# Layer 0's opening: keys first, values and the next keys placed behind the scores

## Chip, core and metric

The kernel runs on one core of one Trainium2 chip. The time is device microseconds for one launch of the whole program; before the change the median of three runs was 2810.7 us (2809.99 to 2813.46).

## What is computed

`x` is 4096 x 256, `adj` is 4096 x 4096, all float32. Four layers follow each other, and after each of them `x` becomes the layer norm of `x` plus the layer's output. The change touches layer 0 alone, an attention with four heads whose scores get the adjacency as a bias and as a mask:

```python
qkv = x @ Wqkv + bqkv                         # 256 -> 3 * 256, then q, k, v
scores = jnp.einsum('hnd,hmd->hnm', qh, kh) * SCALE
scores = scores + graph_bias * adj_matrix[None, :, :]
scores = jnp.where(attn_mask[None, :, :] == 0, jnp.float32(-1000000000.0), scores)
attn = jax.nn.softmax(scores, axis=-1)        # attn_mask is adj as well
out = jnp.einsum('hnm,hmd->hnd', attn, vh)
x = _layernorm(x + (out @ Wout + bout), axis=-1)
```

Layer 1 is a graph attention, layers 2 and 3 are products with the normalised adjacency.

## The kernel before

**Tiles.** Layer 0 goes through 32 row blocks of 128 rows (`Rows`), and for each through two pairs of heads (`Pair`). A pair is a unit; the 4096 keys are four stretches of 1024 columns, so a unit has four steps and the layer 256 (`step(t)`, L462). The program runs in the order in which it is written (`tc.manual_schedule()`, L651): each engine takes its instructions in that order, and what they wait for are semaphores that follow from the data and the buffers.

**A step** issues the scores of unit t // 4, stretch t % 4 (`score`, L361: eight matmul passes into two PSUM tiles, then on VectorE two passes that add the bias, write `z` and keep the maximum, L375); four steps later the exponentials on ScalarE (`expo`, L389); five steps later the transposes on TensorE and their copy out of PSUM on ScalarE (`turn`, L399); six steps later the product with the values (`attend`, L416). So steps 0 to 5 fill a pipeline and the full step begins at t = 6.

**The bias** of the next row block is made beside this, half a tile in a step: `load` (L251) brings a raw tile of 1024 x 128 of `adj` by four DMAs on SP's queue into one of two `raw` buffers; `make_bias` (L264) is three VectorE instructions (transpose, mask, scale and add); `make_edges` (L283) writes the transposed tile as bf16 `mk` (L289, ScalarE, with the row sum; two `mk` buffers) and sends it to DRAM as `edge` from POOL's queue (L295), for layer 1. `fetch` (L299) loads a row block's columns of x transposed, `xq`, and its rows, `xr`; `begin` (L308) makes its queries `qT` (L313 on TensorE, L321 on VectorE).

**Keys and values.** `load_x(mb)` (L197) loads one of eight blocks of 512 columns of x transposed (`xt`, pool of five buffers, which the transposed probabilities use later). `project(mb)` (L204) makes from it the keys of both pairs (L210, eight matmul passes, ScalarE evicts each into `store`, L217) and the values (L226, 16 passes, VectorE adds the bias and evicts, L233), then loads block mb + 4. Keys use the PSUM tiles `po0` and `po1`, one bank each; `begin` uses `po1` too, and the values share the one `tr` tile with the transposes.

**The opening** (L651 to L674) loads x block 0, the key and value weights, raw tile 0 of row block 0, x block 1, raw tile 1, `xq` and `xr`, then two x blocks more; makes the first queries; and then, over four stretches, makes the whole bias of row block 0, with `project(0)` and `project(1)` after the first two. In steps 1, 2 and 3 two further projections, keys and values, stand ahead of the step's score (L478 to L480).

Of the kernel before, what the change touches and what calls it, by code (L numbers as in the profile page):

```python
# [17 lines left out]
N = 4096  # L18
# [8 lines left out]
NS = N // TS  # L27
# [17 lines left out]
def tile_gnn(  # L45
# [123 lines left out]
    with ExitStack() as l0:  # L169
# [25 lines left out]
        x_in = {}  # L195

        def load_x(mb):  # L197
            xt = pp_.tile([P, 2, 512], F32, tag="pt", name="xt")
            nc.sync.dma_start(
                xt, xT[:, mb * 512 : (mb + 1) * 512].rearrange("(c p) m -> p c m", p=P)  # L200
            )
            x_in[mb] = xt

        def project(mb):  # L204

            xt = x_in.pop(mb)
            for pr in range(2):
                pk = ps_o.tile([P, 512], F32, tag=f"po{pr}", name="pk")
                for cc in range(2):
                    nc.tensor.matmul(  # L210
                        pk,
                        wkv_sb[:, cc, pr * P : (pr + 1) * P],
                        xt[:, cc, :],
                        start=(cc == 0),
                        stop=(cc == 1),
                    )
                nc.scalar.activation(  # L217
                    kT[:, pr, mb * 512 : (mb + 1) * 512],
                    pk,
                    AF.Identity,  # L220
                    bias=bqk_sb[:, 2 + pr : 3 + pr],
                )
            pv = ps_t.tile([P, 4, D], F32, tag="tr", name="pv")
            for s in range(4):
                for cc in range(2):
                    nc.tensor.matmul(  # L226
                        pv[:, s, :],
                        xt[:, cc, s * P : (s + 1) * P],
                        wkv_sb[:, cc, D : 2 * D],
                        start=(cc == 0),  # L230
                        stop=(cc == 1),
                    )
            nc.vector.tensor_tensor(  # L233
                v_sb[:, mb * 4 : (mb + 1) * 4, :],
                pv,
                bv_b.unsqueeze(1).to_broadcast([P, 4, D]),
                ALU.add,
            )
            if mb + 4 < N // 512:
                load_x(mb + 4)  # L240

        class Rows:

# [212 lines left out]
        rows = [Rows(ib) for ib in range(NCH)]  # L456
# [5 lines left out]
        def step(t):  # L462
            unit, k = divmod(t, NS)
            ib, pr = divmod(unit, 2)
            live = t < n_steps
            ua, ka = divmod(t - LA, NS)
            tag_a, tag_o = f"po{ua % 2}", f"po{1 - ua % 2}"
            ut, kt = divmod(t - LT, NS)
            ue, ke = divmod(t - LE, NS)
            attends = 0 <= ua < n_units  # L470
            turns = 0 <= ut < n_units
            expos = 0 <= ue < n_units
            grow = live and ib + 1 < NCH
            if grow and pr == 0 and k == NS - 1:
                rows[ib + 1].fetch()
            if ua > 0 and ka == 0:
                pairs[ua - 1].scale()
            if t > 0:  # L478
                for mb in range(2 * t, min(2 * t + 2, N // 512)):
                    project(mb)  # L480
            if live:
                if k == 0:
                    pairs[unit] = Pair(rows[ib], pr)
                pairs[unit].score(k)
            if expos:
                pairs[ue].expo(ke, 0)
            if turns:
                pairs[ut].turn(kt, 0)
            if expos:
                pairs[ue].expo(ke, 1)  # L490
            if attends:
                pairs[ua].attend(ka, tag_a)
                if ka == NS - 2:
                    pairs[ua].sums()
                if ka == NS - 1:
                    pairs[ua].norm(tag_o)
            if ua > 0 and ka == 1:
                if ua % 2 == 0:
                    pairs[ua - 1].rows.finish(tag_o)
                del pairs[ua - 1]  # L500
            if grow:
                if pr == 1 and k == NS - 2:
                    rows[ib + 1].begin(tag_o if attends else "po1")
                kb, half = divmod(pr * NS + k, 2)
                if edges:
                    edges.pop().make_edges()
                edges.append(rows[ib + 1])
                rows[ib + 1].make_bias(kb, half)
                if half == 0 and kb + 1 < NS:
                    rows[ib + 1].load(kb + 1)  # L510
                elif half == 0 and ib + 2 < NCH:
                    rows[ib + 2].load(0)
            elif edges:
                edges.pop().make_edges()
            if turns:
                pairs[ut].turn(kt, 1, by_dve=not live)
            for f, *args in tail.get(t, ()):
                f(*args)
# [98 lines left out]
        def first_es():  # L617
# [30 lines left out]
                (first_es,),  # L648
            ],
        }  # L650
        with tc.manual_schedule():  # L651
            load_x(0)
            nc.sync.dma_start(wkv_sb, wqkv[:, D:].rearrange("(c p) e -> p c e", p=P))
            rows[0].load(0)
            load_x(1)
            rows[0].load(1)
            rows[0].fetch()
            load_x(2)
            load_x(3)
            nc.scalar.dma_start(wout_sb, wout.rearrange("(c p) e -> p c e", p=P))  # L660
            nc.scalar.dma_start(bout_b, bout.partition_broadcast(P))
            rows[0].begin("po1")
            for k in range(NS):
                for half in range(2):
                    rows[0].make_bias(k, half)
                    rows[0].make_edges()
                if k < 2:
                    project(k)
                if k + 2 < NS:
                    rows[0].load(k + 2)  # L670
                elif k + 2 == NS:
                    rows[1].load(0)
            for t in range(n_steps + LA + 2):
                step(t)  # L674

# [446 lines left out]
```

## Time and profile before

| what | value |
|---|---|
| median of three runs | 2810.7 us (2809.99 to 2813.46) |
| the profiled execution's own time | 2810.3 us |
| its span, first to last instruction | 2808.5 us |
| TensorE busy | 2740.4 us (98%) |
| VectorE busy | 2234.3 us (80%) |
| ScalarE busy | 1615.1 us (58%) |
| POOL busy | 234.2 us (8%) |
| mean granted TensorE clock | 0.991 |
| SP, raw tile piece, 128 KB: issue to landing | 3.9 us median over the run, 2.7 to 6.7 in the first 90 us |
| SP, x block, 512 KB: issue to landing | 5.3 us median, 4.4 to 6.0 |

Times come from one profiled execution, in microseconds from the first instruction. The granted clock is the share of TensorE's full speed. `PE` is TensorE's matmuls, `PEld` its weight loads, `DVE` is VectorE, `ACT` ScalarE, `SPq` the issue of DMAs by SP. In a timeline the bracket at the end of a line is the idle time of the engine before it, and who ended it. The chain of waits is followed back from the last instruction to what released it, and so on to the start. Matmul passes are counted one by one: one float32 product in the program is two of them.

### The profile page before, as it was taken

To read this page: it belongs to the slowest core of one execution; us is meant where nothing else is said; L and a number is where in the kernel's file an instruction comes from. 1 tells how busy PE (TensorE), PEld (TensorE's weight loads), DVE (VectorE), ACT (ScalarE), POOL (GpSimd) and SP (SyncE) were. 2 spreads that over 40 slices of the span, in tenths; PEclk is the share of its full clock that TensorE was granted. 3 is DMA by queue.
4 is the path that set the end of the run, shared out by engine and by line. 5 is a ranking of instruction groups with operands and counts; after the bars stand their busy time and mean duration, and the time that the engine had idled before them with its cause. 6 is when DMAs were issued, how large, how long until landed. Compare 5 with 4: busy or idle time off the path is not lost.

```text
span 2808.5 us, 58032 instructions
## 1 busy us (share of the span) xinstructions
PE 2740.4 (98%) x23664; PEld 1870.2 (67%) x23664; DVE 2234.3 (80%) x4091; ACT 1615.1 (58%) x2483; POOL 234.2 (8%) x404
## 2 busy tenths in 40 slices
PE   6999999999999999999998999999999999999997
PEld 4677777777777777777777888887444444444443
DVE  4799999999898999999758888885876568666565
ACT  2699999999999999999855655653100001000000
POOL 1111111111111111111100000000200000000000
PEclk9999999999999999999998999999999999999999
DMA  6344444444444444444362222212555545555552
GB/s 157 61 86 85 87 92 85 88 86 88 90 87 82 90 91 82 86 92 89 100 188 68 76 73 70 76 46 72 177 157 173 163 154 163 164 160 179 180 169 76
DMA packets 671291, 308.01 MB, mean 110 GB/s; under 512 B 547376, under 2 KB 577456, under 8 KB 671024
## 3 DMA queue, kind: packets, MB, share of 16 engines
q1 hardware_dynamic: 655776, 265.10, 38.4%
q0 software_dynamic: 13440, 37.77, 3.5%
q8 instruction: 185, 3.03, 0.5%
q10 hardware_dynamic: 1808, 1.44, 0.2%
q14 instruction: 82, 0.67, 0.1%
HBM read 258.21 MB, written 46.01 MB: 108 GB/s over the span
## 4 chain that ended last, share of the span: by engine, by line
PE 96%; DVE 2%; ACT 1%; DMA 1%; issue 1%; SPq 0%; DVEq 0%; ACTq 0%
PE m L950 27%; PE po L423 17%; PE po L775 16%; PE sc L366 16%; PE ptr L405 10%; PE py L984 2%; PE pq L313 1%; PE pp L335 1%; PE pb L441 1%; PE pk L210 1%; PE pv L226 1%; PE sc L137 1%; PE pm L744 0%; SPq L256 0%; DMA xt<-in_xT 0%
## 5 line engine op out<-in xcount | busy, mean ns | idle before, releaser
L375 DVE CUSTOM_DVE_ANT_0 z<-sc,bias 128x1024 f32<-128x1024 f32 x512 | 605.8, 1220 | 40.5 <-PE sc L366 38.9
L391 ACT ACTIVATE z<-z,nm 128x1024 f32<-128x1024 f32 x512 | 590.2, 1153 | 6.7 <-DVE nm L387 6.7
L413 ACT COPY pt<-ptr 128x1024 f32<-128x1024 f32 x507 | 511.3, 1008 | 99.2 <-PE ptr L405 89.3
L366 PE MATMUL sc<-store,qT 64*128 64x512 f32 x2048 | 507.0, 608 | 1.4 <-DVE mx L375 1.3
L423 PE MATMUL po<-pt,xc 128*64 128x128 f32 x8192 | 504.1, 276 | 0.0
L775 PE MATMUL po<-store,pt 128*128 128x257 f32 x2048 | 459.5, 382 | 3.6 <-DVE pt L765 3.6
L423 PEld LDWEIGHTS po<-pt,xc 128*64 128x64 f32 x8192 | 442.1, 137 | 17.6 <-DVE pt L411 0.2
L405 PEld LDWEIGHTS ptr<-ident,z 64*128 64x128 f32 x8192 | 322.3, 138 | 177.6 <-issue 78.4
L775 PEld LDWEIGHTS po<-store,pt 128*128 128x128 f32 x2048 | 385.0, 190 | 62.9 <-issue 3.6
L950 PE MATMUL m<-asum,ysum 128*128 128x512 f32 x768 | 357.0, 595 | 6.3 <-issue 6.3
L405 PE MATMUL ptr<-ident,z 64*128 64x64 f32 x8192 | 356.5, 225 | 5.8 <-ACT pt L413 4.4
L366 PEld LDWEIGHTS sc<-store,qT 64*128 64x128 f32 x2048 | 192.9, 189 | 119.7 <-issue 109.4
L950 PEld LDWEIGHTS m<-asum,ysum 128*128 128x128 f32 x768 | 146.1, 190 | 177.9 <-issue 160.2
L950 PE MATMUL m<-asum,store 128*128 128x512 f32 x512 | 263.1, 596 | 0.0
L724 ACT ACTIVATE z<-z,es_q 128x1024 f32<-128x1024 f32 x128 | 147.1, 1149 | 183.2 <-DVE mx L711 178.9
L950 PE MATMUL m<-a,ysum 128*128 128x512 f32 x512 | 245.3, 592 | 0.0
L295 POOL DMA_DIRECT2D edge<-mk x256 | 145.3, 568 | 1004.5 <-ACT mk L289 981.0
L956 ACT COPY e<-m 128x512 f32<-128x512 f32 x32 | 18.5, 586 | 351.3 <-PE m L950 351.3
L919 DVE TENSOR_TENSOR asum<-a 128x512 f32<-128x512 f32 x128 | 88.0, 687 | 163.7 <-PE m L950 163.7
L278 DVE SCALAR_TENSOR_TENSOR bias<-rt,gb,u 128x512 f32<-128x512 f32 x256 | 194.1, 758 | 9.1
L950 PEld LDWEIGHTS m<-asum,store 128*128 128x128 f32 x512 | 97.8, 191 | 123.6 <-issue 121.9
L272 DVE STREAM_TRANSPOSE rt<-raw 128x512 f32<-128x512 f32 x256 | 179.6, 702 | 0.0
(126 smaller groups left out, 2544.5 us busy)
## 6 DMA issues: line engine op xcount, KB each, us to landing
a<-in_adjT SPq DMA_DIRECT2D x256, 512.0 KB, 5.1
raw<-in_adjT SPq DMA_DIRECT2D x512, 128.0 KB, 3.9
edge<-mk POOLq DMA_DIRECT2D x256, 128.0 KB, 2.5
mk<-edge SPq DMA_DIRECT2D x256, 128.0 KB, 2.9
xt<-in_xT SPq DMA_DIRECT2D x8, 512.0 KB, 5.3
xq<-in_xT SPq DMA_DIRECT2D x32, 128.0 KB, 3.8
xr<-in_x SPq DMA_DIRECT2D x32, 128.0 KB, 3.0
x<-xs POOLq DMA_DIRECT2D x8, 512.0 KB, 4.0
```

The source lines that it names most:

```text
L272: nc.vector.transpose(rt.rearrange("p (b r) -> p b r", r=QB), self.raw_now[:, half * nb : (half + 1) * nb, :],)
L278: nc.vector.scalar_tensor_tensor(self.bias[k][:, m0 : m0 + HT], rt, gb, u, ALU.mult, ALU.add)
L295: nc.gpsimd.dma_start(edge[self.ib * P : (self.ib + 1) * P, k * TS + m0 : k * TS + m0 + HT], mk)
L366: nc.tensor.matmul(ps[j][:, q * 512 : (q + 1) * 512], self.rows.qT[j * HD : (j + 1) * HD, self.pr, :], kT[j * HD : (j + 1) * HD, self.pr, ...
L375: nc.vector.tensor_tensor_reduce(z, ps[j], self.rows.bias[k], 1.0, NEG, ALU.add, ALU.max, self.mx[:, j, k : k + 1],)
L391: nc.scalar.activation(z, z, AF.Exp, bias=self.nm[:, j : j + 1], accum_out=self.ls[:, j, k : k + 1],)
L405: nc.tensor.transpose(pa[:, r, c, :], z[half, c * P : (c + 1) * P], ident[half, half])
L413: nc.scalar.copy(to, pa)
L423: nc.tensor.matmul(self.po[j * HD : (j + 1) * HD, 0:P], v_sb[:, ci, h * HD : (h + 1) * HD], self.pt[j][k][:, c, :], start=(ci == 0), stop= ...
L724: nc.scalar.activation(self.z[s], self.z[s], AF.Prelu, bias=self.eq[:, s : s + 1], alpha=SLOPE)
L775: nc.tensor.matmul(self.po[:, 0 : D + 1], self.pt[:, b, :, :].rearrange("p s i -> p (s i)"), wh[:, b, :], start=(b == 0), stop=(b == NBK - 1),
L950: nc.tensor.matmul(self.m[i], left, right, start=(c == 0), stop=(c == NP - 1))
```

## The change

`project` is cut into `project_k` and `project_v`. The opening's DMAs are put in another order: `xq` and `xr` go ahead of x block 1 and raw tile 1, and all of the first five x blocks are loaded ahead of the first computation. Before step 0 stand only the keys of block 0, the first queries, the keys of block 1 and the bias of stretch 0. A table `plan` gives what steps 0 to 4 do behind their score: in steps 0, 1 and 2 the values of two blocks, the keys of the two next and the next stretch of row block 0's bias, in turn; in steps 3 and 4 the values of block 6 and of block 7. Each block's load follows the values five blocks before it. Raw tiles 2 and 3 of row block 0 and tiles 1 and 2 of row block 1 are loaded at other places in these steps. From step 4 on the loads of raw tiles are where they were, and from step 5 on a step issues what it did.

```diff
-        def project(mb):
-            xt = x_in.pop(mb)
+        def project_k(mb):
+            xt = x_in[mb]
             for pr in range(2):
                 pk = ps_o.tile([P, 512], F32, tag=f"po{pr}", name="pk")
...
+        def project_v(mb):
+            xt = x_in.pop(mb)
             pv = ps_t.tile([P, 4, D], F32, tag="tr", name="pv")
...
-            if mb + 4 < N // 512:
-                load_x(mb + 4)
+            if mb + 5 < N // 512:
+                load_x(mb + 5)
...
-            if t > 0:
-                for mb in range(2 * t, min(2 * t + 2, N // 512)):
-                    project(mb)
             if live:
                 if k == 0:
                     pairs[unit] = Pair(rows[ib], pr)
                 pairs[unit].score(k)
+            for f, *args in plan.get(t, ()):
+                f(*args)
...
                 rows[ib + 1].make_bias(kb, half)
-                if half == 0 and kb + 1 < NS:
+                if t < NS:
+                    if t == 1:
+                        rows[0].load(3)
+                    if 0 < t < 3:
+                        rows[1].load(t)
+                elif half == 0 and kb + 1 < NS:
                     rows[ib + 1].load(kb + 1)
...
+        def first_bias(k, half):
+            rows[0].make_bias(k, half)
+            rows[0].make_edges()
+            if k == 1 and half == 1:
+                rows[0].load(2)
+
+        plan = {}
+        for t in range(3):
+            plan[t] = [
+                (project_v, 2 * t),
+                (project_k, 2 * t + 2),
+                (first_bias, t + 1, 0),
+                (project_v, 2 * t + 1),
+                (project_k, 2 * t + 3),
+                (first_bias, t + 1, 1),
+            ]
+        plan[3] = [(project_v, 6)]
+        plan[4] = [(project_v, 7)]
         with tc.manual_schedule():
             load_x(0)
             nc.sync.dma_start(wkv_sb, wqkv[:, D:].rearrange("(c p) e -> p c e", p=P))
             rows[0].load(0)
+            rows[0].fetch()
             load_x(1)
             rows[0].load(1)
-            rows[0].fetch()
-            load_x(2)
-            load_x(3)
+            for mb in range(2, 5):
+                load_x(mb)
...
+            project_k(0)
             rows[0].begin("po1")
-            for k in range(NS):
-                for half in range(2):
-                    rows[0].make_bias(k, half)
-                    rows[0].make_edges()
-                if k < 2:
-                    project(k)
-                if k + 2 < NS:
-                    rows[0].load(k + 2)
-                elif k + 2 == NS:
-                    rows[1].load(0)
+            project_k(1)
+            for half in range(2):
+                rows[0].make_bias(0, half)
+                rows[0].make_edges()
+            rows[1].load(0)
             for t in range(n_steps + LA + 2):
                 step(t)
```

## The prediction

> **What bounds the kernel now.** The page came first: TensorE is busy 98% of the span. But an average hides stages, so next I read the windows view (columns: stretch, its length, busy us and instructions of PE, PEld, DVE, ACT, POOL; then granted TensorE clock, DMA share, GB/s).
>
> ```profile
> PE 2740.4 (98%) x23664; PEld 1870.2 (67%) x23664; DVE 2234.3 (80%) x4091; ACT 1615.1 (58%) x2483; POOL 234.2 (8%) x404
> ...
> 0.00:10.00 10.00, 0.00 (x0) 0.00 (x0) 0.23 (x1) 1.28 (x1) 0.74 (x7) 1.00 0.72 198
> 10.00:20.00 10.00, 0.00 (x0) 0.00 (x0) 0.00 (x0) 0.00 (x0) 0.00 (x0) 1.00 1.10 177
> ...
> 90.00:100.00 10.00, 9.16 (x32) 4.11 (x30) 9.06 (x16) 4.85 (x9) 0.54 (x1) 0.66 0.37 66
> ...
> 210.00:1300.00 1090.00, 1090.00 (x15526) 823.82 (x15520) 994.78 (x1938) 1019.41 (x1679) 164.91 (x288) 1.00 0.43 87
> ```
>
> From 210 to 1300 us TensorE never pauses, so work before that loop moves the end one for one. Ahead of it stand 20 us in which TensorE does nothing while the DMA engines are full, and a stretch around 95 with few matmuls at 0.66 clock. What holds TensorE is told by the chain of waits, TensorE's timeline and SP's queue (start, duration, what).
>
> ```profile
> 0.75 5.75 DMA xt<-in_xT
> ...
> 16.34 3.62 DMA xq<-in_xT
> ...
> 20.01 2.08 PE pq L313 x8
> 22.09 4.05 PE pk L210 x8
> 26.14 3.45 PE pv L226 x16
> 29.59 3.43 PE pk L210 x8
> ...
> 41.33 4.71 DMA edge<-mk
> ```
>
> ```profile
> 47.49 3.70 PE L210 MATMUL pk<-xt,wkv_sb 128*128 128x512 f32 x8 [2.01 <-ACT store L217]
> ...
> 86.35 1.99 PE L366 MATMUL sc<-store,qT 64*128 64x512 f32 x8
> 89.65 8.55 PE L366 MATMUL sc<-store,qT 64*128 64x512 f32 x15 [1.32 <-DVE mx L375]
> ...
> 100.88 1.94 PE L366 MATMUL sc<-store,qT 64*128 64x512 f32 x8
> 102.99 0.71 PE L405 MATMUL ptr<-ident,z 64*128 64x64 f32 x16 [0.17 <-ACT pt L413]
> ```
>
> ```profile
> 5.63 5.43 SPq L256 DMA_DIRECT2D raw<-in_adjT  x4
> 11.11 0.85 SPq L199 DMA_DIRECT2D xt<-in_xT  x1
> 12.00 4.30 SPq L256 DMA_DIRECT2D raw<-in_adjT  x4
> 16.34 0.90 SPq L302 DMA_DIRECT2D xq<-in_xT  x1
> 17.28 0.47 SPq L306 DMA_DIRECT2D xr<-in_x  x1
> ```
>
> To see: the first matmul (query projection `pq`) waits for `xq`, issued behind eight raw pieces, although x block 0 was there at 6.50 and `wkv_sb` at 7.9 (issued 1.24, 6.7 to landing). Then everything is one chain of matmuls up to the fourth score at 86.35, broken once for 2.01 us: ScalarE's `mk` waited for an edge write and held the key eviction behind it. All eight value projections (3.45 each) stand ahead of that fourth score. After it TensorE waits for VectorE and ScalarE: the 13.3 us from 89.65 to 102.99 hold three scores (3 x 1.94) and two sets of transposes (2 x 0.71), some 7 us of work.
>
> [...] `pq` took 2.08 cold (1.16 at 105.52) and the clock stood at 0.50 from 91.5 to 98.3. [...]
>
> **The change, part by part.**
> *SP's order.* `xq` and `xr` pass x block 1 and row 0's raw tile 1. `xq` issues at 11.11 and with the same 3.62 lands at 14.73. Block 1 issues at 11.11 + 0.90 + 0.47 + two pauses of 0.04 = 12.56. The fastest block takes 4.4, the median 5.3, the slowest 6.0: 16.96 to 18.56. In the old trace it landed at 16.02, 1.68 after the raw tile ahead of it; `xq` and `xr` are half as many bytes, which makes 16.86 behind them. I take 17.2. The five x blocks and two raw tiles still end near 24.8, as before; block 2 is needed only at 26.
> *Keys first.* `project_k(0)` starts at 7.95. It is cold: its first two matmuls took 1.69 in the old run, so at worst 8 x 0.845 = 6.8, to 14.7, and its second eviction (0.69) ends near 15.4, which `pq` awaits (same PSUM bank). `pq` ends at 15.9 (warm, at 14.73) to 17.4. Either way `project_k(1)` starts when its block is there, 17.2 (17.4 at worst). Score 0 follows 3.45 later, at 20.65. VectorE has from 16.0 for qT (0.6) and two bias halves (1.87 each): 20.4, ahead of the end of score 0 at 22.6.
> *One opening step* keeps the same TensorE work: two keys (2 x 3.43 and 0.2 once), two values (2 x 3.45), a score (1.92) = 15.9, as from 70.46 to 86.35. Three steps put score 3 at 20.65 + 47.7 = 68.3: 18.05 earlier. Cross-check: start 2.8 earlier, `pq` and one key block out of the way 2.08 + 4.05, two values deferred 6.9, the stall 2.0, rounding 0.2.
> *What must stay hidden in a step.* VectorE gains two bias halves: 2.3 (scores) + 2.4 (values) + 3 x 1.87 = 10.3 of 15.9. ScalarE: four evictions and three `mk`, about 5. A late raw tile first delays the bias half between the two value evictions; the second eviction has 4.8 us to spare there. Raw tile 3 of row 0 now issues only when row 1's first tile is read (about 52.8), behind x block 7 in SP's queue, which asks for `project_v(2)`, long done. Its last piece goes out 1.8 later and takes 3.9 to 6.7: 58.5 to 61.3, wanted at 59.1. Up to 2.2 late, covered by the 4.8; uncovered it would cost 2.2. Row 1's tiles have 6 us or more. `make_edges` moves too: POOL's edge writes are spread out, so the 2.01 stall has nothing to cause it; three `mk` in a row return at 67 to 70 with two buffers, and what queues behind them is the first exponential, which waits for the maximum at 72.7 anyway. Uncovered: about 2.
> *Filling with two values left.* Score 3 ends 70.2; value 6 to 73.65; score 4 to 75.6; value 7 to 79.05. VectorE: z 3 to 72.6, value 6 added to 74.9, bias to 76.8, z 4 to 79.1, value 7 to 80.3, bias to 82.2, z 5 to 84.5. Score 5 to 81.0, first transposes to 81.7, ScalarE's copy to 82.7, second transposes to 83.4; score 6 waits for z 5 in its second bank, ends about 86.0. The next transposes, 102.99 before, start at 86.1: 16.9 earlier. So the deferred 6.9 us cost about 1.1; the half clock should not return, since TensorE is now fed through there.
> *Sum.* From there the instructions are the same in the same order, and the loop is TensorE's. 2810.3 (this profiled execution, span 2808.5 and 1.8 around it) - 16.9 = 2793.4. It stood 0.4 under the median of the runs, 2810.7; on the median's scale 2793.8.
>
> **Rivals.**
> A. The deferred values show in full, because VectorE's chain z, value, bias, z decides the filling (it has no pause in my working from 73.7 on): 18.05 - 6.9 = 11.2 gained, 2799.5. Against: the old filling had 6 us of TensorE idle to take them.
> B. The clock stays low through the broken opening (TensorE idles perhaps 14.7 to 14.8 and 15.9 to 17.2): `project_k(1)` and score 0 at half speed add up to 5.4: 2797 to 2799. Against: 2.01 us idle at 45.5 did not drop it.
> C. Raw tiles late beyond cover, twice about 2: 2797.8. Against: the 4.8.
> D. Slower: the loop settles in another phase. ScalarE (1019 of 1090) and VectorE (995) are near their bound, so a fill that hands over with other slack could leave a short TensorE wait in each step. Some 250 steps follow; 16.9 / 250 = 0.07 us a step cancels the gain, 0.1 makes 25 - 16.9: 2819. Against: the loop's own order resets the phase, and 1090 us without a pause show no such wait.
> E. It does not do what it says to the end: the opening is earlier, but loads that do not follow hold the first loop steps; 2809.
>
> **How the numbers follow.** A measurement of this kernel tells about 0.2% (5.6 us) from no change. Forecast 62% (2790.5 to 2797), A 15%, B 10%, C 5%, D 4%, E 4%. Faster: A, B, C and the forecast, 0.92; same 0.04; slower 0.04. Low end: block 1 at 16.96 and nothing given back in the filling is 18.3, two us more for what the timeline may hide: 2790; high end A. That leaves out D, E and the tails.
>
> **What would show it.** Right: first matmul `pk` near 8; `pq` near 14.7; score 0 at 20.65, score 3 near 68; no eviction wait near 45; full clock at 70 to 90; the loop at 100% as before. Wrong: score steps longer than 15.9 with VectorE waiting for `raw` (C), doubled matmul times after 15 (B), gaps before scores 4 to 6 (A), pauses in the loop (D).

## The result and the profile after

| what | before | after |
|---|---|---|
| median of the runs (four each) | 2810.6 us (2810.0 to 2813.5) | 2792.6 us (2791.7 to 2793.5) |
| the profiled execution's own time | 2810.3 us | 2793.5 us |
| its span | 2808.5 us | 2791.7 us |
| mean granted TensorE clock | 0.991 | 0.992 |
| fourth score (score 3) starts | 86.35 | 68.31 |
| queries of row block 1 (`pq`) start | 105.52 | 90.84 |

The ratio is 0.993, with the interval 0.9918 to 0.9943: faster by more than the 0.2% that a measurement tells from no change. The forecast was 2793.8 us. What stands behind the cut `project` lies four lines further down (the scores' L366 is L370, the queries' L313 is L317).

First the page's engine line of the changed kernel and its windows (stretch, its length, busy us and instructions of PE, PEld, DVE, ACT, POOL; granted clock, DMA share, GB/s).

```profile
PE 2737.4 (98%) x23664; PEld 1867.9 (67%) x23664; DVE 2235.6 (80%) x4091; ACT 1614.4 (58%) x2483; POOL 233.7 (8%) x404
...
0.00:10.00 10.00, 2.13 (x3) 1.13 (x4) 0.23 (x1) 1.28 (x1) 0.73 (x7) 1.00 0.72 199
10.00:20.00 10.00, 8.27 (x21) 3.65 (x21) 3.77 (x8) 2.06 (x3) 0.73 (x1) 1.00 1.22 188
...
84.70:88.20 3.50, 3.50 (x11) 1.40 (x11) 3.43 (x6) 2.06 (x4) 1.28 (x2) 0.51 0.36 75
210.00:1283.00 1073.00, 1073.00 (x15266) 811.02 (x15264) 979.84 (x1909) 1001.99 (x1652) 161.94 (x283) 1.00 0.43 87
```

The engine totals hardly moved; the change took waiting away, not work. The first 20 us, empty before, now hold 10.4 us of matmuls. The loop is still TensorE's without a pause. And one stretch runs at half clock, at 84.7: a thing the forecast said should not return. TensorE's timeline of the same kernel (start, duration, what, count; in brackets the idle time before it and who ended it) and below it SP's queue:

```profile
7.87 6.25 PE L210 MATMUL pk<-xt,wkv_sb 128*128 128x512 f32 x8 [7.87 <-DMA wkv_sb<-in_wqkv]
14.90 1.16 PE L317 MATMUL pq<-xq,w_sb 128*128 128x128 f32 x8 [0.78 <-ACT store L217]
17.01 3.70 PE L210 MATMUL pk<-xt,wkv_sb 128*128 128x512 f32 x8 [0.96 <-DMA xt<-in_xT]
20.64 1.99 PE L370 MATMUL sc<-store,qT 64*128 64x512 f32 x8
...
68.31 1.99 PE L370 MATMUL sc<-store,qT 64*128 64x512 f32 x8
...
83.03 0.71 PE L409 MATMUL ptr<-ident,z 64*128 64x64 f32 x16 [1.10 <-ACT pt L417]
83.84 4.07 PE L370 MATMUL sc<-store,qT 64*128 64x512 f32 x7
...
90.84 1.16 PE L317 MATMUL pq<-xq,w_sb 128*128 128x128 f32 x8
```

```profile
10.80 0.84 SPq L306 DMA_DIRECT2D xq<-in_xT  x1
11.69 0.47 SPq L310 DMA_DIRECT2D xr<-in_x  x1
12.20 0.43 SPq L199 DMA_DIRECT2D xt<-in_xT  x1
```

To see: the first matmul starts with the weights, 12.1 us earlier than the first of before; the queries wait 0.78 for the second key eviction and the second block's keys 0.96 for their block, which SP issued behind `xq` and `xr`; then there is no bracket until the filling, and the 2.01 us stall on an eviction is gone. Score 3 starts 18.04 earlier. From there to the queries of row block 1 the old kernel took 105.52 - 86.35 = 19.17 us and the new one 90.84 - 68.31 = 22.53: the filling gives 3.36 back, and the loop starts 14.68 earlier. In the loop the lead stays between 14.66 and 14.71. So 16.8 at the end needs another 2.1, and the traces place 1.6 of it near the end of layer 0. TensorE's timeline there, before:

```profile
1380.56 0.71 PE L405 MATMUL ptr<-ident,z 64*128 64x64 f32 x16 [2.00 <-ACT pt L413]
1381.11 3.13 PE L366 MATMUL sc<-store,qT 64*128 64x512 f32 x8
...
1386.95 0.71 PE L405 MATMUL ptr<-ident,z 64*128 64x64 f32 x16
```

and after, the same three instructions of the program:

```profile
1365.86 0.71 PE L409 MATMUL ptr<-ident,z 64*128 64x64 f32 x16 [1.99 <-ACT pt L417]
1366.41 1.94 PE L370 MATMUL sc<-store,qT 64*128 64x512 f32 x8
...
1370.66 0.71 PE L409 MATMUL ptr<-ident,z 64*128 64x64 f32 x16
```

Both kernels stop for 2.0 us at this point. Before, the score after it took 3.13 instead of 1.94, since the clock stood at half from 1381.7 to 1385.1; after, it did not. The lead is 1380.56 - 1365.86 = 14.70 ahead of these lines and 1386.95 - 1370.66 = 16.29 behind them. The last 0.5 comes in two steps, where layers 1 and 2 begin: the lead is 1485.51 - 1469.23 = 16.28 at the first large product of layer 1, 1958.53 - 1941.91 = 16.62 at the first product of layer 2 and 1962.03 - 1945.23 = 16.80 a few products later. At both places the clock of both kernels stands at half (granted 0.50), and before it does so for longer behind the same product: 5.4 us against 4.7 (to 1490.9 and 1474.0), and 3.4 against 3.1 (to 1962.0 and 1945.0). At half clock the work lost is half of these differences, which is the 0.34 and 0.18 of the two steps.

### The profile page after: what moved, and what is told of

Its sections match the earlier page's. It is cut to its first block, busy times and chain, and to the rows that moved or that the text cites. A ratio compares the mean times of both kernels' runs of the same rounds, so it can differ in the third digit from the quotient of the medians.

```text
span 2791.7 us, 58032 instructions
## 1 busy us (share of the span) xinstructions
PE 2737.4 (98%) x23664; PEld 1867.9 (67%) x23664; DVE 2235.6 (80%) x4091; ACT 1614.4 (58%) x2483; POOL 233.7 (8%) x404
## 4 chain that ended last, share of the span: by engine, by line
PE 96%; DVE 2%; DMA 1%; ACT 1%; issue 0%; SPq 0%; DVEq 0%; ACTq 0%
PE m L975 27%; PE po L427 17%; PE po L800 16%; PE sc L370 16%; PE ptr L409 11%; PE py L1009 2%; PE pp L339 1%; PE pq L317 1%; PE pb L445 1%; PE pv L230 1%; PE pk L210 1%; PE sc L137 1%; DMA xt<-in_xT 0%; PE pm L769 0%; SPq L260 0%
## 5 line engine op out<-in xcount | busy, mean ns | idle before, releaser
L370 PE MATMUL sc<-store,qT 64*128 64x512 f32 x2048 | 503.6, 605 | 0.1
L370 PEld LDWEIGHTS sc<-store,qT 64*128 64x128 f32 x2048 | 192.2, 189 | 117.7 <-issue 111.7
```

Source lines behind the costliest of these rows:

```text
L370: nc.tensor.matmul(ps[j][:, q * 512 : (q + 1) * 512], self.rows.qT[j * HD : (j + 1) * HD, self.pr, :], kT[j * HD : (j + 1) * HD, self.pr, ...
```

## The experiments

My theory after the result: the gain at the loop's start is the sum of four parts, queries' data earlier, keys of block 0 in the wait for it, the stall removed, and two values moved into the filling, less what the filling gives back, part of which is clock. The rivals were that a single part (the early `xq`) carries all, that the deferred values show in full, and that the filling is late for ScalarE's sake. Each run was compared with the kernel before on the same chip. The third and fourth columns are starts in the profiled execution; the last says how far the loop's start lies behind that of the changed kernel (negative: ahead).

| run | median us | ratio to before (interval) | score 3 | `pq` of row block 1 | behind after |
|---|---|---|---|---|---|
| e1_xq_early | 2805.18 | 0.9984 (0.9977 to 0.999) | 80.97 | 100.23 | 9.39 |
| e2_key0_first | 2805.0 | 0.998 (0.9973 to 0.9987) | 82.35 | 101.52 | 10.68 |
| e3_no_deferral | 2802.49 | 0.9972 (0.9963 to 0.9982) | 76.91 | 97.17 | 6.33 |
| e5_xq_late | 2798.36 | 0.9959 (0.9946 to 0.9971) | 73.62 | 94.60 | 3.76 |
| e6_after_again | 2793.04 | 0.994 (0.9927 to 0.9952) | 70.29 | 91.27 | 0.43 |
| e8_value0_early | 2790.07 | 0.9927 (0.9915 to 0.994) | 66.50 | 87.48 | -3.36 |
| e4_pair1_keys_later | 2791.06 | 0.9933 (0.9919 to 0.9946) | 65.14 | 87.78 | -3.06 |
| e9_filler | 2794.91 | 0.9947 (0.9934 to 0.9959) | 68.27 | 90.59 | -0.25 |
| e11_no_deferral_spaced | 2799.56 | 0.9963 (0.995 to 0.9975) | 75.13 | 94.29 | 3.45 |
| e12_queries_first | 2796.78 | 0.9948 (0.9936 to 0.9961) | 72.81 | 93.78 | 2.94 |
| e10_both | 2789.41 | 0.9921 (0.9908 to 0.9935) | 62.70 | 85.35 | -5.49 |

The first four shared a chip (before: 2809.42), the next four another (2810.76), the last three a third (2809.76). Since the kernel before differs by up to 1.3 us between the chips, so may any two medians from different chips.

**e1_xq_early: the old kernel with SP's order alone.**

```diff
             rows[0].load(0)
+            rows[0].fetch()
             load_x(1)
             rows[0].load(1)
-            rows[0].fetch()
```

> The kernel before with one edit: xq and xr are loaded ahead of x block 1 and raw tile 1. My theory (TensorE's chain sets the opening, and its first link is xq): the first matmul starts near 14.5 instead of 20.0, and the time falls by 5.0 to 5.5, to about 2805.4. Rival (the opening is paced by raw tiles, VectorE's bias and the mk behind them): the stall near 45, 2.0 us before, grows by what was gained, and the time falls by 3 or less.

The queries start at 14.90, 5.1 earlier, and the loop 5.3 earlier; 4.2 us by the medians, where 5.0 to 5.5 was forecast. The eviction stall did not grow with the earlier start, it is 1.73:

```profile
42.11 3.70 PE L210 MATMUL pk<-xt,wkv_sb 128*128 128x512 f32 x8 [1.73 <-ACT store L217]
```

So SP's order alone is worth a quarter (medians) to a third (loop's start) of the whole, and all of it lasts through the loop: no load behind it takes it back.

**e2_key0_first: e1, and the keys of block 0 ahead of the queries.**

```diff
+            project_k(0)
             rows[0].begin("po1")
...
-                if k < 2:
-                    project(k)
+                if k == 0:
+                    project_v(0)
+                if k == 1:
+                    project(1)
```

> The run above with a second edit: the keys of block 0 stand ahead of the first queries; the bias of row block 0 is still made in one go ahead of step 0, and nothing else is deferred. My theory: TensorE starts near 7.9 and reaches score 0 about 10 us earlier, but then waits longer for ScalarE, whose mk of the last stretches and the key evictions behind them follow the raw tiles: a stall of 4 to 5 us where 2.0 stood, so 7 to 8 gained, about 2803. Rival (keys first is all there is to it): 10 gained, 2800.5.

Both forecasts of the time missed: against e1 it is worth nothing (0.2 by the medians, 1.3 lost at the loop's start). The stall of 4 to 5 us did come. TensorE now starts at 7.91, but then:

```profile
28.14 1.13 PE L374 MATMUL sc<-store,qT 64*128 64x512 f32 x4 [1.05 <-ACT store L217]
...
40.81 6.38 PE L210 MATMUL pk<-xt,wkv_sb 128*128 128x512 f32 x8 [4.46 <-ACT store L217]
```

The bias of row block 0 is still made in one piece, so the evictions of keys queue on ScalarE behind `mk`. Ahead of the wait of 1.05 `mk` waits for an edge write (5.90, then 0.59). Ahead of that of 4.46 it waits for VectorE's transposed tile (3.91), and VectorE waits for the raw tile (2.88):

```profile
36.80 0.71 DVE L280 STREAM_TRANSPOSE rt<-raw 128x512 f32<-128x512 f32 x1 [2.88 <-DMA raw<-in_adjT]
```

TensorE only reaches these waits earlier: 1.05 and 4.46 where e1 had 1.73. Then the clock is at half (0.50) from 39.4 to 46.2, and the keys behind the long wait take 6.38 where e1's take 3.70, another 2.7. A head start is worth nothing when what it runs into has not moved.

**e3_no_deferral: the changed kernel with the values of blocks 6 and 7 at the end of step 2.**

```diff
-        plan[3] = [(project_v, 6)]
-        plan[4] = [(project_v, 7)]
+        plan[2] += [(project_v, 6), (project_v, 7)]
```

> The changed kernel with the values of blocks 6 and 7 put back ahead of score 3, at the end of step 2. My theory: score 3 comes 6.9 us later, of which the filling behind it gives back some 3.4 (score 3 to the queries of row block 1 took 19.2 before and 22.5 after), so about 3.5 slower than the changed kernel, 2796.1. Rival A of the prediction (the deferred values show in full): no difference, 2792.6. A third way, that the filling hid them wholly: 6.9 slower, 2799.5.

Missed by 6: my edit made a wait of its own. Two value projections back to back share one PSUM tile, so the second waited 1.32 for VectorE's eviction (`xc`) of the first. That is not all of it: the filling took 20.26 where I had 19.2, and this execution has a half-clock stretch at the end of layer 0 (1373.5 to 1376.9). The run can't say what the deferral alone is worth; e11 below repeats it without that wait.

**e5_xq_late: the changed kernel with `xq` and `xr` back behind raw tile 1.**

```diff
             rows[0].load(0)
-            rows[0].fetch()
             load_x(1)
             rows[0].load(1)
+            rows[0].fetch()
```

> The changed kernel with xq and xr back behind x block 1 and raw tile 1. My theory: the keys of block 0 still start near 7.9, but the queries start near 19.9 and the keys of block 1 near 21.1 instead of 17.0, with nothing to make up for it: 4.1 slower than the changed kernel, 2796.7. Rival (the order of SP's queue is worth nothing once the keys go first, since later steps have slack): no difference.

The queries fall back to 19.97 and score 0 to 25.96, 5.3 later, as does score 3. At the loop's start 3.8 of it remain: this execution had its half clock in the opening (16.2 to 23.0), and its filling takes 20.98 where that of the changed kernel's first profile takes 22.53. The median is 1.7 over the forecast; between it and that of e6, which ran on another chip, lie 5.3. The early `xq` is worth about as much here as in e1.

**e6_after_again: the changed kernel itself, in five runs.**

> The changed kernel unaltered, to stand on the same chip beside the three below. 2791.5 to 2793.5, 17 to 18 under the kernel before.

It repeats the gain (17.7 by the medians). Its profiled execution shows what no edit made, one window of e6 (columns as above):

```profile
17.70:21.10 3.40, 3.40 (x5) 1.35 (x4) 2.27 (x4) 0.34 (x1) 0.00 (x0) 0.50 0.96 223
```

and the line of TensorE's timeline that it slows:

```profile
17.30 5.40 PE L210 MATMUL pk<-xt,wkv_sb 128*128 128x512 f32 x8 [1.64 <-DMA xt<-in_xT]
```

The program is the same, but the half clock fell into the opening and not into the filling. The keys of block 0 took 5.16 instead of 6.25, so the two waits behind them are longer than in the first profile: 1.50, for `xq`, and 1.64 instead of 0.78 and 0.96. The keys of block 1 start 0.29 later and take 5.40 instead of 3.70, so score 3 comes 1.98 later. The filling takes 20.98 instead of 22.53. Up to score 6 the two fillings run alike (15.53 from score 3 to score 6 in both), so the difference, 1.55, is what the half clock cost the filling in the first profile.

**e8_value0_early: values of block 0 in the wait for `xq`.**

```diff
+        del plan[0][0]
...
             project_k(0)
+            project_v(0)
             rows[0].begin("po1")
```

> The changed kernel with the values of block 0 put between the keys of block 0 and the first queries, where TensorE waited 0.8 and 0.96 us for xq and x block 1. My theory (the opening up to score 3 is TensorE's chain): 3.45 us of work fill 1.75 us of waiting, so score 3 and the end come 1.7 us earlier. Rival (what follows the queries, VectorE's bias of stretch 0, decides score 0's successor): no gain.

More than expected: 3.0 under e6. From the first line to the filling TensorE's timeline of this kernel has no further bracket:

```profile
7.93 6.65 PE L210 MATMUL pk<-xt,wkv_sb 128*128 128x512 f32 x8 [7.93 <-DMA wkv_sb<-in_wqkv]
14.42 3.62 PE L230 MATMUL pv<-wkv_sb,xt 128*128 128x256 f32 x16
17.87 1.05 PE L317 MATMUL pq<-xq,w_sb 128*128 128x128 f32 x8
18.76 3.60 PE L210 MATMUL pk<-xt,wkv_sb 128*128 128x512 f32 x8
```

The two waits of the changed kernel, 0.78 + 0.96 = 1.74, are filled with work that was ready: score 3 comes 1.8 earlier. The other 1.55 of the 3.36 at the loop's start is the clock, full through this execution's filling (20.98 us, as in e6). No run shows that the edit did that, since e6 had it without the edit. The 3.0 of the medians lies between the waits filled, 1.74 in the first profile and 3.14 in e6.

**e4_pair1_keys_later: the second pair's keys of blocks 6 and 7 in step 5.**

```diff
-        def project_k(mb):
+        def project_k(mb, prs=(0, 1)):
...
-            for pr in range(2):
+            for pr in prs:
...
-                (project_k, 2 * t + 2),
+                (project_k, 2 * t + 2, (0, 1) if t < 2 else (0,)),
...
+        gaps = {(5, 0): [(project_k, 6, (1,))], (5, 1): [(project_k, 7, (1,))]}
```

The entries of `gaps` run behind the first and second transposes of step 5; the second half of step 2's keys is cut in the same way.

> The changed kernel with the second pair's keys of blocks 6 and 7 (3.4 us of TensorE, not needed before step 7) taken out of step 2 and put in step 5, behind the first and the second transposes. My theory (between score 3 and the queries of row block 1 TensorE has some 4 us that VectorE's and ScalarE's chain leaves free, in part at half clock): score 3 comes 3.4 earlier, VectorE's bias halves in the shortened step take back some 1.3, the half clock of 84.7 to 88.2 goes: 2 to 3.5 faster than the changed kernel. Rival (TensorE's own work fills that stretch): no difference.

As expected: 2.0 under e6, loop 3.06 earlier. The holes at 81.9 and before score 6 now hold matmuls, the clock stays full, and score 6 takes 1.99. The filling takes 22.64. Against the first profile with its half clock it gives back 0.1 of the 3.17 gained at score 3; against a filling at full clock, 20.98, it gives back 1.66. So it had room for about half of this work.

The run also bears on what keeps the clock up. In the first profile the 3.41 us ahead of the fall, which begin 13.02 us behind score 3 (81.33 to 84.74), held 2.20 us of matmuls, and then the clock was at half for 3.42. At the same place behind score 3 (78.2 to 81.6) this execution holds 3.26, and the clock stays at 1.00.

**e9_filler: four matmuls that nobody reads, two behind each transpose of step 5.** Nothing is left out of the computation.

```diff
                 pairs[ut].turn(kt, 0)
+            if t == LT:
+                busy()
```

and the same behind `turn(kt, 1)`.

> The changed kernel with two times two matmuls more in step 5 (1.7 us in all, into a PSUM tile that nothing reads), behind the first and the second transposes: work that is no use but to keep TensorE busy. Theory (the low clock of 84.7 to 88.2 came because TensorE had too little to do in the 3.4 us before it, and it doubled the time of score 6): no half clock there, score 6 back from 4.1 to 2, and although work is added the loop starts 1 to 2 us earlier. Rival (score 6 was slow because it waits for VectorE's z 5; the clock is no cost): the same time or up to 1.7 slower.

The clock is full where it was at half (this kernel's line for 84.7 to 88.2):

```profile
84.70:88.20 3.50, 3.50 (x16) 1.31 (x16) 2.59 (x5) 2.02 (x3) 1.28 (x2) 1.00 0.36 74
```

and score 6 takes 1.99 instead of some 4: the loop starts 0.25 earlier although matmuls were added. They are more than the 1.7 us expected. Each of the four is two passes, and TensorE's timeline has

```profile
81.81 1.98 PE L668 MATMUL pf<-store 128*128 128x512 f32 x4
...
84.37 1.98 PE L668 MATMUL pf<-store 128*128 128x512 f32 x4
```

about 3.8 us in all, part of it in what were waits. Against a filling at full clock (20.98) this one, 22.32, is 1.34 longer. That fits the clock as a cost of the filling, but does not prove it: the points of the grid on which an execution's clock changes (measured further down, where the prediction is gone through) lie here at 11.0 and 14.4 us behind score 3, as they do in e5 (10.9 and 14.3), whose clock stayed up without a filler. As an improvement it missed: 1.9 over e6 by the medians. An execution in which the clock would have stayed up anyway only pays for the filler.

**e11_no_deferral_spaced: e3 without its own wait.** Step 2 does all four values, with keys between any two.

```diff
+        plan[2] = [
+            (project_v, 4),
+            (project_k, 6, (0,)),
+            (project_v, 5),
+            (project_k, 6, (1,)),
+            (first_bias, 3, 0),
+            (project_v, 6),
+            (project_k, 7, (0,)),
+            (project_v, 7),
+            (project_k, 7, (1,)),
+            (first_bias, 3, 1),
+        ]
```

with the lines of `plan[3]` and `plan[4]` dropped.

> The changed kernel with the values of blocks 6 and 7 back in step 2, this time with keys between any two values, so that no values wait for the eviction of those before. My theory (deferred values are hidden in the filling but for what score 3 to the queries of row block 1 grows by, 19.2 to 21.0 without and 22.5 with a half clock): score 3 is 6.9 later, the loop starts 4.5 to 5.5 later, 2797.5 to 2798.5. The prediction's own working (of the 6.9 deferred, 1.1 is given back): 5.8 later. Rival A (the deferral shows in full): no difference from the changed kernel.

Score 3 comes 6.82 later (two values, 2 x 3.45 = 6.9), the loop 3.45 later: of the 6.8 us deferred, half is hidden and half given back in the filling. My forecast, 4.5 to 5.5 later, missed. Both executions have one half-clock stretch in the filling (80.3 to 83.7 here), but it does not weigh on both alike: this filling takes 19.16, and the same one in the kernel before, with 6.8 us at half clock instead of 3.4, takes 19.17. Against the deferred filling at full clock (20.98) only 1.8 is given back and 5.0 is hidden. The prediction's working had 5.8 hidden of 6.9; rival A had none. The medians say more: each against before on its own chip, the gain is 10.2 without the deferral and 17.7 to 18.0 with it. That is over 7, more than was deferred, so the spread of the medians or something else is in it; this execution has a half-clock stretch at the end of layer 0 too (1370.5 to 1373.9).

**e12_queries_first: the changed kernel with the queries ahead of the keys of block 0.**

```diff
-            project_k(0)
             rows[0].begin("po1")
+            project_k(0)
             project_k(1)
```

> The changed kernel with the first queries ahead of the keys of block 0. My theory: TensorE starts near 14.9 instead of 7.9, cold, with 2.05 of queries and 4.2 of keys before the keys of block 1, which start near 21.0 instead of 17.0, so score 0 and the end come 3.9 later, 2797.0. Rival (keys first is worth nothing, as it was worth nothing when it was put into the kernel before beside an early xq, 2805.0 against 2805.2): 2793.0.

The time is as expected: 2796.78 where 2797.0 was written down. The queries start at 14.64, and take 2.05, where those of the first profile, behind the keys, take 1.16; score 0 starts at 25.14, 4.50 later where 3.9 was forecast. 2.94 of it is left at the loop's start, since this filling takes 20.97 at full clock; in the medians against e6, on another chip, it is 3.7. So the order that was worth nothing in the old arrangement (e2) is worth 3 to 4 us in the new one, where the bias is made in pieces and no eviction stands in its way.

**e10_both: e8 and e4 together.** Their edits are as above.

> The changed kernel with both edits that made it faster alone: the values of block 0 ahead of the queries (3.0 faster than the changed kernel beside it) and the second pair's keys of blocks 6 and 7 in step 5 (2.0 faster). My theory (each takes away another piece of TensorE's waiting): they add up, 4.5 to 5 faster than the changed kernel, 2788. Rival (both mend the same thing, the clock that falls in one gap or the other): no faster than the better of the two, 2790.

The fastest median of the study, 2789.41, between the theory (2788) and the rival (2790): TensorE is busy 29.86 of the 30 us from 60 to 90, and the loop starts 5.49 earlier than in the changed kernel. But its execution has a half-clock stretch at 1361.5 to 1364.9, so less arrives at the end than at the loop's start, and against e8 (2790.07, another chip) the time can't be told apart. Whether the two edits add up stays open.

## Why the prediction was right, and where it was not

**The start and the keys.** Predicted: first matmul 7.95, queries 14.7 to 15.4, block 1's keys 17.2, score 0 20.65. Measured: 7.87, 14.90, 17.01, 20.64. The wait of the queries was the one named, for the second key eviction; in e3, e6 and e9 the eviction was done earlier and `xq` ended the wait. e12 shows that keys first is a real part of it, e5 and e1 that the early `xq` is. Adding SP's own issue times to the old issue-to-landing time gave the landing of block 1 within 0.3 us, although the queue was reordered. The DMA share in the second 10 us is 1.22 where it was 1.10. Of what went back in SP's queue, x block 1 (issued at 12.20 instead of 11.11) kept its keys waiting 0.96, and for raw tile 1 (12.68 instead of 12.00) no wait is shown.

**The step.** Predicted 15.9, measured 15.89 three times over: 20.64, 36.53, 52.42, 68.31. VectorE's two added bias halves stayed hidden, and there is no stall near 45. The stall's removal has no run of its own; e2 shows what it costs to leave it in. Score 3 at 68.3 was met to 0.01, which is partly luck: e6, the same kernel, has it at 70.29.

**Cover.** The forecast let raw tile 3 of row block 0 go out at 52.8 and come up to 2.2 late. It went out at 50.96 and its last piece landed at 56.63, wanted at 59.24. I had it wait for the wrong buffer: the tile takes the one that VectorE's transpose of the tile before frees at 50.9. The three `mk` in a row were priced at nothing because the first exponential waits for a maximum anyway. ScalarE's timeline of the changed kernel:

```profile
74.08 0.63 ACT L293 ACTIVATE mk<-rt 128x512 bf16<-128x512 f32 x1 [3.75 <-DMA edge<-mk]
74.70 1.13 ACT L395 ACTIVATE z<-z,nm 128x1024 f32<-128x1024 f32 x1
```

The third `mk` waited 3.75 for the edge write that frees its buffer, and the exponential behind it started at 74.70, some 1.8 later than it could have. The cover named was too short; what hid it was another, TensorE's own queue, in which the first transposes stand at 81.27 behind values and score 5.

**The filling: the step that failed.** "So the deferred 6.9 us cost about 1.1; the half clock should not return." It cost 3.36. Of that 1.55 is the half clock, which did return (84.7 to 88.2) in the profiled execution, and 1.8 stands where I had 1.1. In the four other executions of this filling (e5, e6, e8, e12) the clock stayed up, at 20.97 or 20.98 us: that it "should not return" is true of most executions, and no more than that. At full clock, as in e6, the transposes ahead of `attend` (all but the first three of sixteen) start 88.37 - 70.29 = 18.08 behind score 3, so at 86.39 on the clock of the forecast, which had 86.1; and the queries of row block 1 follow them after 2.90, where I had taken the old kernel's 105.52 - 102.99 = 2.53 for granted: 0.3 and 0.4. So the working of the engines was near and the clock was the large miss. e11 gives the same answer from the other side: 3.45 of the deferral's 6.8 is kept in this execution, 5.0 at full clock.

**The sum came right because of a second error.** Predicted 16.9 of gain, all of it made before the loop; measured 14.68 there, and 16.8 at the end. 1.59 of the 2.1 between is the half-clock stretch behind the 2.0 us wait at the end of layer 0, which the execution of before had and that of after had not. The other 0.5 is the shorter half clock at the starts of layers 1 and 2. None of the 2.1 is a merit of the change in itself, so the nearness of 16.8 to 16.9 is luck. What a median gains on the clock's account is not fixed by these two executions.

**Where that stretch comes from** could be read from the profiles together (granted clock in slices of 0.2 us). In the first 2000 us of the execution of before the clock is at half (0.50) from 91.47 to 98.30, 1381.71 to 1385.12, 1473.87 to 1490.94 and 1955.15 to 1961.98. These are 6.83, 3.41, 17.07 and 6.83 us, or two, one, five and two times 3.413, and between them lie 376.0, 26.0 and 136.0 times that length. In that of after they are 3.42 us from 84.74, 17.07 from 1456.90 and 6.83 from 1938.18, with 401.0 and 136.0 times 3.413 between. So within these executions the changes of the clock lie on a grid of 3.413 us, and my reading takes one change to fix the grid of any execution here. Every kernel here has the same wait of 1.99 or 2.00 us at the end of layer 0. In seven executions (before, e1, e2, e3, e9, e10, e11) it lies wholly between two neighbouring points of the grid, and the clock is at half for the next 3.41 us in all seven; in five of them an earlier fall, 378.0 times 3.413 us before, fixes the same grid, in e9 and e10 this fall alone does. In three others (after, e5, e6) a point of the grid cuts the wait, and the clock stays at 1.00: into 0.86 and 1.13 (after), 0.26 and 1.73 (e5), 1.64 and 0.36 (e6). In e4, e8 and e12 the clock stays at 1.00 there as well; where their grid lies is not shown. TensorE was not idle all through the 3.42 us ahead of such a fall: in before they hold 1.42 us of matmuls at the end of layer 0, and 2.07 of 3.41 ahead of the fall at 91.47. This is a reading of thirteen executions, not an experiment: no run removed that wait. And the matmuls between two points of the grid do not decide it alone: the clock fell at 84.74 in the changed kernel after 2.20 us of them and stayed up in e6 after 2.22, between two points that lie 0.8 us sooner in the program. Nor does the reading explain all of the medians: gain in medians and gain at the loop's start differ by up to 3.5 us among the runs, and the runs of before spread over 5.4 us on one chip and 8.4 on another.

**The rivals.** A (values in full, 2799.5) fell, though half of it happened in the first profile: 3.4 of 6.8 show, 1.8 at full clock. B (half clock in the opening) did not happen in the first profile and did in e6, where it cost 1.7 at the keys of block 1; the 3.42 us ahead of it, 14.28 to 17.70, hold the end of the first wait named for it, all of the second (1.64), and only 1.53 us of matmuls. That filling then ran 1.55 shorter at full clock, so little of it is left at the loop's start. The reason given against B, that 2.01 us idle at 45.5 did not drop the clock, was weak: a point of that execution's grid, at 47.1, cuts the wait into 1.6 and 0.4. C fell, since the raw tile was early. D fell: the lead of 14.7 holds through the 1073 us, where the rival needed a drift of 0.07 per step. E fell. That the filling is late for ScalarE's sake got no run of its own; its one wait on ScalarE there is the 1.10 before the second transposes, in e6 as in the first profile.

## What to carry to other kernels

A moved step has no worth of its own: keys ahead of the queries gave 0.2 us in the old arrangement and 3 to 4 in the new one, so find what the earlier engine runs into next (here an eviction queued behind an instruction that waits, directly or through VectorE, for a DMA) and move that first. Compare two traces at a few named instructions from start to end rather than at the end alone: here the loop's start showed 14.7, the end 16.8, and the difference belonged to the clock. Fill a short wait at the start with any work that is ready: the values of block 0 gave 1.8 us at score 3 and 3.0 by the medians. Whether such an edit also moves what the clock does later is not shown.

## What was not expected of the hardware

At the end of layer 0 a wait of 2.0 us was followed by 3.41 us at half of TensorE's clock whenever it lay whole between two points of the 3.413 us grid on which the changes of the clock lie (seven executions); cut by such a point, even as 0.26 and 1.73, it was not (three; in three more the clock stayed up and the grid is not shown). Such a stretch cost 1.6 us at the end of layer 0 and 1.55 in the filling. The same kernel shows the stretch in different places from one execution to the next (17.7 in e6, 84.7 in the first profile), and one profile of a change of this size can be off by one or two of these.
